# Seven products instead of eight in a feed-forward, inside a pipelined two-layer graph kernel

## The chip, the cores and the metric

The kernel runs on one core of one Trainium2 chip. Its engines each work through a queue of their own: TensorE (PE; its weight loads are shown apart as PEld), VectorE (DVE), ScalarE (ACT), GpSimd (POOL) and SyncE (SP), which here only issues transfers. They wait for each other by semaphores. TensorE writes its results into PSUM, eight banks of 128 partitions x 512 float32; the other engines read them from there. The metric is the device time of one execution in microseconds (us), as the median of several runs.

## The reference: two layers over 64 small graphs

The input is `x` of 64 x 256 x 256 (batch, node, feature) and an integer adjacency `adj` of 64 x 256 x 256. The first layer is two graph attentions, a norm, a feed-forward with Relu, and a norm. The second is attention with eight heads weighted by relation, a norm, a feed-forward with Gelu, and a norm. Cut to what the change touches:

```python
# first layer (weights of layer 0)
h = gat(gat(x, adj, W1, a1), adj, W2, a2)      # softmax over masked scores, then a product
h = layernorm(x + h)
ff = relu(h @ w_ff1 + b_ff1) @ w_ff2 + b_ff2    # 256 -> 1024 -> 256
x = layernorm(h + ff)
# second layer (weights of layer 1)
# ... queries, keys, scores, relation-weighted values ...
x = _ln(src + attn_out, g1, beta1)
ff = jax.nn.gelu(x @ W1 + b1, approximate=False) @ W2 + b2   # x @ W1 is what changes
return _ln(x + ff, g2, beta2)
```

All of it is in float32. The product `x @ W1` is 16384 x 256 by 256 x 1024.

## The kernel before

The batches are taken two at a time: 32 groups of 512 tokens. A turn of the loop works on three groups at once, each at another stage: `y_` is in the second layer, `x_` in the first layer's feed-forward, `z` in the graph attention. The order of TensorE's and SyncE's instructions is the order of the program text; for the other engines a scheduler picks it when the kernel is built. Blocks of 128 tokens are numbered t = 0 to 3, P = 128, F = N = 256, FF = 1024, KB = NB = G = 2, T = 4, FB = 8, TN = 512. `bank()` gives one of six PSUM banks.

The pieces concerned (cuts are marked):

```python
def normed_features(u, l, xn, natural=False, queues=(nc.sync,)):
    # features onto partitions: transposes in 32x32 squares, then 16 placing transfers
    yt = work.tile([P, Q, KB, T, 32], F32, tag="yt", name=f"yt{u}_{l}", bufs=1)
    for t in range(T):
        nc.vector.transpose(yt[:, :, :, t].rearrange("p q k r -> p k q r"),
                            xn[:, t].rearrange("p (k q c) -> p k q c", k=KB, c=32))
    # ... natural: another layout of the same, 16 transfers on SyncE's queue ...
    hT = work.tile([P, Q, KB, T, 32], F32, tag="hT", name=f"hT{u}_{l}")
    for q in range(Q):
        for a in range(Q):
            queues[a % len(queues)].dma_start(hT[q * 32:(q + 1) * 32, a], yt[a * 32:(a + 1) * 32, q])
    return [hT[:, :, k].rearrange("p a t r -> p t a r") for k in range(KB)]

def gat_softmax(u, l, wh, c, w, aT):
    rows = bank(f"rows{name}")
    for t in range(T):
        nc.tensor.transpose(rows[:, t * P:(t + 1) * P], wh[:, t, c:c + 1].to_broadcast([P, P]), ident)
    # ...
    for b in range(G):
        for t in range(b * NB, (b + 1) * NB):
            nc.scalar.activation(s[:, t, :], rows[:, b * N:(b + 1) * N], AF.Identity, bias=wh[:, t, c + 1:c + 2])
        sb = s[:, b * NB:(b + 1) * NB, :].rearrange("p t n -> p (t n)")
        nc.vector.scalar_tensor_tensor(sb, sb, ALPHA, sb, op0=ALU.mult, op1=ALU.max)
        nc.scalar.activation(sb, sb, AF.Exp)
        for t in range(b * NB, (b + 1) * NB):
            nc.vector.scalar_tensor_tensor(s[:, t, :], s[:, t, :], 1.0, aT[:, t, :], op0=ALU.mult, op1=ALU.mult,
                                           accum_out=z[:, t:t + 1])
    nc.vector.reciprocal(z, z)
    # ...
    for t in range(T):
        nc.scalar.activation(wh[:, t, :w], wh[:, t, :w], AF.Copy, scale=z[:, t:t + 1])
    return s

def gat_first(u, s, xp):                        # products hpp
    for t in range(T):
        # ... two matmuls of 258 columns into a bank ...
        nc.scalar.copy(hp[:, t, :WH], ps[:, :WH])

def normed(u, l, y, blocks=range(T)):
    # ...
    for t in blocks:
        nc.vector.bn_stats(st[:, t, :], y[:, t, :])
        nc.vector.bn_aggr(mv[:, t, :], st[:, t, :])
    nc.gpsimd.tensor_scalar(rs[:, bt], mv[:, bt, 1], EPS, 0.0, op0=ALU.add, op1=ALU.add)
    nc.gpsimd.tensor_tensor(rs[:, bt], rs[:, bt], mhalf[:, bt], ALU.pow)
    nc.vector.scalar_tensor_tensor(nm[:, bt], mv[:, bt, 0], -1.0, rs[:, bt], op0=ALU.mult, op1=ALU.mult)
    for t in blocks:
        nc.scalar.activation(y[:, t, :], y[:, t, :], AF.Identity, bias=nm[:, t:t + 1], scale=rs[:, t:t + 1])
    # ...

def affine(y, g_, b_):
    nc.vector.tensor_mul(y, y, g_[:, None, :].to_broadcast(list(y.shape)))
    nc.vector.tensor_add(y, y, b_[:, None, :].to_broadcast(list(y.shape)))

def hidden(u, l, hT, wi, bi, func, blocks, h1=None):   # h1p: 8 banks a group, 2 matmuls of 512 columns each
    # ...
    for f in blocks:
        ps = bank(f"h1p{u}_{l}_{f}")
        for k in range(KB):
            nc.tensor.matmul(ps, wi[:, k, f * P:(f + 1) * P], hT[k], start=(k == 0), stop=(k == KB - 1))
        nc.scalar.activation(h1[:, f, :], ps, func, bias=bi[:, f:f + 1])
    return h1
```

`hidden_out` and `hidden_out_block` are the second product of a feed-forward (`yfp`): per block of tokens 8 matmuls of 256 columns, and after two blocks VectorE adds the bank to `y`. The second half of a turn:

```python
    # ... attention of y_, first_hidden of x_ in between; load_x(z + 1) ...
    out_(0)
    piece()
    if Z:
        project(z)
    out_(1)
    if Z:
        first_scores(z)                      # rows and the first softmax
    normed(y_, 2, y)
    if X:
        hT = normed_features(y_, 2, y, queues=(nc.sync, nc.scalar))
        affine(X["y"], rg1, rb1)
    else:
        piece()
        hT = to_features(y, f"h3T{y_}")
    affine(y, rg3, rb3)
    if X:
        hidden_out(x_, 0, X["y"], X["h1"], wf2)
        normed(x_, 1, X["y"])
    if waiting:
        finish(*waiting.pop(), 0, G)         # the output norm of the group before, and its transfer
    if Z:
        checked(z, Z["aq"])
    if z + 1 < NG:
        load_adjacency(z + 1)
    if Z:
        Z["hp"] = gat_first(z, Z["s"], Z["xp"])
    h1 = hidden(y_, 1, hT, w1, b1, AF.Gelu, range(FB))
    if X:
        X["hT"] = (normed_features(x_, 1, X["y"], natural=True) if Z else to_features(X["y"], f"h2T{x_}"))
        affine(X["y"], rg2, rb2)
    if Z:
        second_scores(z)                     # rows and the second softmax
    # ... the last two turns put off the rest ...
    for t in range(T):
        if t == T - 1:
            second_sums(z)
        hidden_out_block(y_, 1, y, h1, w2, t)
    waiting.append((y_, y))
```

Of the kernel before, what the change touches and what calls it, by code (L numbers as in the profile page):

```python
# [16 lines left out]
P = 128  # L17
# [368 lines left out]
def narrow_path(  # L386
# [171 lines left out]


# [9 lines left out]
    def scaled(w, scale):  # L569
        for k in range(KB):  # L570
            nc.gpsimd.tensor_scalar(w[:, k], w[:, k], scale[:, k:k + 1], 1.0, op0=ALU.mult, op1=ALU.mult)

    def folding():

        shifted(wf1, range(FB // 2), lb1, bf1, "bf1")
        yield
        shifted(wf1, range(FB // 2, FB), lb1, bf1, "bf1")
        scaled(wf1, lg1)
        yield
        for w, bias, name in ((wq, bq, "bq"), (wk, bk, "bk")):  # L580
            shifted(w, range(KB), lb2, bias, name)
            scaled(w, lg2)
        yield
        ps = bank("rbvp")
        for k in range(KB):
            nc.tensor.matmul(ps, lb2[:, k:k + 1].to_broadcast([P, P]), wv[:, k].rearrange("p r f -> p (r f)"),
                             start=(k == 0), stop=(k == KB - 1))
        nc.vector.tensor_tensor(rbv, rbv, ps, ALU.add)
        scaled(wv.rearrange("p c r f -> p c (r f)"), lg2)
        shifted(w1, range(FB // 2), lb3, b1, "b1")  # L590
        yield
        shifted(w1, range(FB // 2, FB), lb3, b1, "b1")
        scaled(w1, lg3)
        yield
# [6 lines left out]


# [16 lines left out]
    def normed_features(u, l, xn, natural=False, queues=(nc.sync,)):  # L619


        yt = work.tile([P, Q, KB, T, 32], F32, tag="yt", name=f"yt{u}_{l}", bufs=1)
        for t in range(T):
            nc.vector.transpose(yt[:, :, :, t].rearrange("p q k r -> p k q r"),  # L624
                                xn[:, t].rearrange("p (k q c) -> p k q c", k=KB, c=32))
        if natural:
            hT = work.tile([P, KB, TN], F32, tag="hT", name=f"hT{u}_{l}")
            to = hT.rearrange("c k (t a r) -> c (k t) a r", a=Q, r=32)
            for q in range(Q):
                for a in range(Q):  # L630
                    nc.sync.dma_start(to[q * 32:(q + 1) * 32, :, a],
                                      yt[a * 32:(a + 1) * 32, q].rearrange("c k t r -> c (k t) r"))
            return [hT[:, k] for k in range(KB)]
        hT = work.tile([P, Q, KB, T, 32], F32, tag="hT", name=f"hT{u}_{l}")
        for q in range(Q):
            for a in range(Q):
                queues[a % len(queues)].dma_start(hT[q * 32:(q + 1) * 32, a], yt[a * 32:(a + 1) * 32, q])
        return [hT[:, :, k].rearrange("p a t r -> p t a r") for k in range(KB)]
# [29 lines left out]
    def gat_softmax(u, l, wh, c, w, aT):  # L668

        name = f"{u}_{l}"  # L670
        rows = bank(f"rows{name}")
        for t in range(T):
            nc.tensor.transpose(rows[:, t * P:(t + 1) * P],  # L673
                                wh[:, t, c:c + 1].to_broadcast([P, P]), ident)
        s = work.tile([P, T, N], F32, tag="s", name=f"s{name}")
        z = work.tile([P, T], F32, tag="z", name=f"z{name}")
        for b in range(G):
            for t in range(b * NB, (b + 1) * NB):
                nc.scalar.activation(s[:, t, :], rows[:, b * N:(b + 1) * N], AF.Identity,  # L679
                                     bias=wh[:, t, c + 1:c + 2])  # L680
# [9 lines left out]
        for t in range(T):  # L690
            nc.scalar.activation(wh[:, t, :w], wh[:, t, :w], AF.Copy, scale=z[:, t:t + 1])
        return s

    def gat_first(u, s, xp):
        hp = work.tile([P, T, WX], F32, tag="wh", name=f"hp{u}")
        for t in range(T):
# [19 lines left out]
    def normed(u, l, y, blocks=range(T)):  # L716
# [14 lines left out]
        for t in blocks:  # L731
            nc.scalar.activation(y[:, t, :], y[:, t, :], AF.Identity, bias=nm[:, t:t + 1],  # L732
                                 scale=rs[:, t:t + 1])
# [8 lines left out]
    def hidden(u, l, hT, wi, bi, func, blocks, h1=None):  # L742
# [9 lines left out]
        return h1  # L752

# [103 lines left out]

    def first_scores(z):
        d = g[z]
        d["s"] = gat_softmax(z, 0, d["xp"], F + 2, WH, d["aT"])  # L860

    def second_scores(z):
        d = g[z]
        d["s"] = gat_softmax(z, 1, d["hp"], F, F, d["aT"])
# [24 lines left out]
    def finish(u, y, b, n):  # L889
# [3 lines left out]
        affine(y[:, bt, :], rg4, rb4)  # L893
# [6 lines left out]
    def turn(y_, x_, z):  # L900
# [52 lines left out]
        if Z:  # L953
            first_scores(z)
        normed(y_, 2, y)
        if X:
            hT = normed_features(y_, 2, y, queues=(nc.sync, nc.scalar))
            affine(X["y"], rg1, rb1)
        else:
            piece()  # L960
            hT = to_features(y, f"h3T{y_}")
        affine(y, rg3, rb3)
        if X:
            hidden_out(x_, 0, X["y"], X["h1"], wf2)
            normed(x_, 1, X["y"])
        if waiting:
            finish(*waiting.pop(), 0, G)
# [4 lines left out]
        if Z:  # L972
            Z["hp"] = gat_first(z, Z["s"], Z["xp"])
        h1 = hidden(y_, 1, hT, w1, b1, AF.Gelu, range(FB))
        if X:
            X["hT"] = (normed_features(x_, 1, X["y"], natural=True) if Z
                       else to_features(X["y"], f"h2T{x_}"))
            affine(X["y"], rg2, rb2)
        if Z:
            second_scores(z)  # L980
        if y_ >= NG - 2:
# [100 lines left out]
```

## Time and profile before

| | before |
|---|---|
| median of three runs | 3218.24 us (3218.14 to 3224.62) |
| profiled execution, span | 3218.0 us |
| mean granted TensorE clock | 0.994 |
| instructions | 44167 |

In the profile, a group of instructions is named by line, engine, operation and the tiles it writes and reads, as `h1p<-hT,w`: the product `h1p` from features `hT` and weights `w`. `128x512` is partitions by elements. "[1.62 <-POOL rs L728]" means that the engine sat idle for 1.62 us before, and that GpSimd's write of `rs` at line 728 ended the wait. Times in a timeline are from the start of the span, and several instructions in a row are merged, with their count as `x8`. An instruction that only issues a transfer stands under SPq or ACTq. Matmuls overlap, so a row's duration reaches past the start of the next row; from start to start is what a row costs.

Two groups of the page, which are the two feed-forward products of the second layer:

```profile
L760 PE MATMUL yfp<-w,h 128*128 128x256 f32 x2048 | 452.9, 379 | 0.0
...
L749 PE MATMUL h1p<-hT,w 128*128 128x512 f32 x992 | 430.8, 592 | 0.0
```

After the names come the count, the busy time in us and the mean of one in ns, and the engine's idle time before them.

### The profile page before, as it was taken

How to read it: one execution, taken by the hardware profiler on the slowest of the kernel's cores; microseconds unless marked ns; L12 is line 12 of the kernel's file. 1: busy time of each engine (PE TensorE's matmuls, PEld its weight loads, DVE VectorE, ACT ScalarE, POOL GpSimd, SP SyncE). 2: the span in 40 equal slices, each digit the busy share in tenths (PEclk: the TensorE clock that was granted, in tenths of full speed). 3: DMA queues.
4: the chain of work that ended last, by engine and by line, in shares of the span. 5: the costliest groups of instructions: out<-in, count | busy, mean ns of one | idle time of the engine just before them, and what ended most of it. 6: DMA issues, size and time to landing. Idle time of an engine off the chain costs nothing.

```text
span 3218.0 us, 44167 instructions
## 1 busy us (share of the span) xinstructions
PE 3175.9 (99%) x16816; PEld 2040.2 (63%) x16816; DVE 1958.3 (61%) x3550; ACT 1432.6 (45%) x2756; POOL 193.6 (6%) x381
## 2 busy tenths in 40 slices
PE   8999999999999999999999999999999999999998
PEld 5566656566666666665666665666666665656655
DVE  3556666555675666665656665566665666655555
ACT  4344444444444444434444444444344444444432
POOL 1000000000000000000000000000000000000000
PEclk9999999999999999999999999999999999999999
DMA  5011111121111221111211112211112111111100
GB/s 143 20 40 40 34 38 33 42 46 31 41 28 40 46 45 29 41 32 40 47 33 40 34 33 46 46 29 42 30 40 46 40 33 38 34 42 34 25 16 15
DMA packets 473050, 125.08 MB, mean 39 GB/s; under 512 B 401368, under 2 KB 472192, under 8 KB 472832
## 3 DMA queue, kind: packets, MB, share of 16 engines
q1 hardware_dynamic: 459520, 112.71, 16.0%
q10 hardware_dynamic: 12256, 8.43, 0.9%
q8 instruction: 136, 2.23, 0.3%
q0 software_dynamic: 1056, 1.05, 0.1%
q14 instruction: 82, 0.67, 0.1%
HBM read 57.04 MB, written 16.78 MB: 23 GB/s over the span
## 4 chain that ended last, share of the span: by engine, by line
PE 97%; DVE 1%; DMA 1%; ACT 0%; POOL 0%; issue 0%; SPq 0%; ACTq 0%; POOLq 0%; DVEq 0%
PE h1p L749 28%; PE yfp L760 27%; PE po L829 7%; PE vp L792 7%; PE sp L808 4%; PE yop L711 4%; PE qp L779 3%; PE xpp L663 3%; PE kp L779 3%; PE hpp L700 3%; PE ygp L711 3%; PE zo L832 2%; PE rows L673 1%; DVE rz L837 0%; ACT y L732 0%; DMA rg<-in_L_gnn_g_ln_dram 0%
## 5 line engine op out<-in xcount | busy, mean ns | idle before, releaser
L816 DVE TENSOR_TENSOR ea<-e,aT 128x1024 f32<-128x1024 f32 x256 | 302.2, 1222 | 333.7 <-ACT e L814 333.7
L751 ACT ACTIVATE h<-h1p,cols 128x512 f32<-128x512 f32 x512 | 338.9, 691 | 348.6 <-PE h1p L749 348.2
L732 ACT ACTIVATE y<-y,nm,rs 128x256 f32<-128x256 f32 x512 | 265.3, 588 | 442.3 <-DVE nm L729 436.4
L760 PE MATMUL yfp<-w,h 128*128 128x256 f32 x2048 | 452.9, 379 | 0.0
L749 PE MATMUL h1p<-hT,wf 128*128 128x512 f32 x992 | 450.6, 602 | 0.0
L760 PE MATMUL yfp<-wf,h 128*128 128x256 f32 x2048 | 447.4, 379 | 0.0
L749 PE MATMUL h1p<-hT,w 128*128 128x512 f32 x992 | 430.8, 592 | 0.0
L760 PEld LDWEIGHTS yfp<-wf,h 128*128 128x128 f32 x2048 | 387.0, 190 | 51.9 <-issue 0.5
L760 PEld LDWEIGHTS yfp<-w,h 128*128 128x128 f32 x2048 | 386.6, 190 | 52.3 <-issue 0.8
L814 ACT ACTIVATE e<-sp 128x512 f32<-128x512 f32 x512 | 263.8, 602 | 224.4 <-PE sp L808 218.0
L749 PEld LDWEIGHTS h1p<-hT,w 128*128 128x128 f32 x992 | 188.4, 190 | 224.2 <-issue 200.7
L749 PEld LDWEIGHTS h1p<-hT,wf 128*128 128x128 f32 x992 | 180.6, 189 | 228.8 <-issue 193.1
L837 DVE RECIPROCAL rz<-zo 128x512 f32<-128x512 f32 x64 | 214.7, 3354 | 53.5 <-PE zo L832 53.5
L682 DVE SCALAR_TENSOR_TENSOR s<-s 128x512 f32<-128x512 f32 x128 | 87.1, 680 | 242.6 <-ACT s L679 241.3
L792 PE MATMUL vp<-wv,hT 128*128 128x512 f32 x480 | 214.0, 599 | 0.0
L624 DVE STREAM_TRANSPOSE yt<-y 128x256 f32<-128x256 f32 x368 | 152.4, 433 | 83.5 <-ACT y L732 77.8
L725 DVE BATCH_NORM_STATS2 st<-y 128x6 f32<-128x256 f32 x512 | 193.2, 409 | 4.4
L739 DVE TENSOR_TENSOR y<-y,rg 128x1024 f32<-128x1024 f32 (+1 forms) x130 | 156.3, 1202 | 9.3 <-ACT y L732 6.0
L792 PEld LDWEIGHTS vp<-wv,hT 128*128 128x128 f32 x480 | 88.7, 190 | 110.4 <-issue 103.2
L740 DVE TENSOR_TENSOR y<-y,rb 128x1024 f32<-128x1024 f32 (+1 forms) x130 | 156.5, 1204 | 3.3
L727 POOL TENSOR_SCALAR rs<-mv 128x4 f32<-128x4 f32 (+1 forms) x130 | 31.1, 248 | 2084.0 <-DVE mv L726 2076.7
L819 DVE TENSOR_TENSOR es<-e 128x1024 f32<-128x1024 f32 x128 | 156.0, 1219 | 0.0
(155 smaller groups left out, 3561.8 us busy)
## 6 DMA issues: line engine op xcount, KB each, us to landing
hT<-yt SPq DMA_DIRECT2D x1224, 32.0 KB, 1.9
y<-in_x_dram SPq DMA_DIRECT2D x32, 512.0 KB, 4.0
xq<-in_x_dram SPq DMA_DIRECT2D x240, 64.0 KB, 2.4
aq<-in_adj_dram SPq DMA_DIRECT2D x240, 64.0 KB, 2.5
out_dram<-y SPq DMA_DIRECT2D x30, 512.0 KB
hT<-yt ACTq DMA_DIRECT2D x248, 32.0 KB, 1.9
wf<-in_L_gnn_w_ff_dram SPq DMA_DIRECT2D x2, 1024.0 KB, 7.1
w<-in_L_gnn_W_dram SPq DMA_DIRECT2D x2, 1024.0 KB
```

The lines of the kernel that those rows point to most:

```text
L711: nc.tensor.matmul(ps[:, i * F:(i + 1) * F], lhs(t, k), rhs(b, k), start=(k == 0), stop=(k == n - 1))
L725: nc.vector.bn_stats(st[:, t, :], y[:, t, :])
L732: nc.scalar.activation(y[:, t, :], y[:, t, :], AF.Identity, bias=nm[:, t:t + 1], scale=rs[:, t:t + 1])
L749: nc.tensor.matmul(ps, wi[:, k, f * P:(f + 1) * P], hT[k], start=(k == 0), stop=(k == KB - 1))
L751: nc.scalar.activation(h1[:, f, :], ps, func, bias=bi[:, f:f + 1])
L760: nc.tensor.matmul(ps[:, i * F:(i + 1) * F], h1[:, k, t * P:(t + 1) * P], wo_[:, k, :], start=(k == 0), stop=(k == FB - 1))
L779: nc.tensor.matmul(ps, w[:, k, m * P:(m + 1) * P], hT[k], start=(k == 0), stop=(k == KB - 1))
L792: nc.tensor.matmul(ps, hT[k][:, t * P:(t + 1) * P], wvf[:, k, :], start=(k == 0), stop=(k == KB - 1))
L814: nc.scalar.activation(e[:, a, :], ps[a], AF.Exp, scale=isd)
L816: nc.vector.tensor_tensor(ea[:, a:a + 2, :], e[:, a:a + 2, :], ab[:, None, :].to_broadcast([P, 2, NB * N]), ALU.mult)
L829: nc.tensor.matmul(po[hp, m * N:(m + 1) * N], vs[:, hp], w[:, a, j * N:(j + 1) * N], start=(n == 0), stop=(n == len(terms) - 1))
L837: nc.vector.reciprocal(rz, zo)
```

## The change

The first product of the second feed-forward is done by Strassen's scheme, in the form with four sums on each side and running totals. The weights (256 x 1024) are cut into quarters by input half and output half, the features (256 x 512) into quarters by input half and batch. Seven products of such quarters and some additions give the four quarters of the result, instead of eight products. The weight sums are made once, by GpSimd, at the start. In each turn VectorE makes four differences of feature quarters; the products go into four PSUM banks (two for each half `h` of an output quarter); ScalarE copies some of the intermediate sums out, VectorE adds them to others on the way to `h1`, and later products are added in the same banks (`start` false). Gelu then works on `h1` in place for three of the quarters. The two matmul groups of `gat_first`, which stood ahead of the product, are put between its last parts.

The rest is order. Instructions inside `behind(name)` are to be issued after the last instruction marked with that name: the first softmax behind the transposes and transfers of the features, the norm of the first feed-forward behind the copies out of the banks, the output norm behind the second softmax. Lastly, GpSimd places the four diagonal blocks of the transposed features, so that 12 transfers are left of 16.

```diff
+    def seven(w, name):
+        h = FF // 2
+        a11, a12, a21, a22 = (w[:, k, o * h:(o + 1) * h] for o in range(2) for k in range(2))
+        s1, s2, s4 = (const.tile([P, h], F32, name=f"{name}s{n}") for n in (1, 2, 4))
+        nc.gpsimd.tensor_tensor(s1, a21, a22, ALU.add)
+        nc.gpsimd.tensor_tensor(s2, s1, a11, ALU.subtract)
+        nc.gpsimd.tensor_tensor(s4, a12, s2, ALU.subtract)
+        nc.gpsimd.tensor_tensor(a21, a11, a21, ALU.subtract)
+        return a11, a12, a22, s1, s2, a21, s4
 ...
         scaled(w1, lg3)
+        w1s.extend(seven(w1, "w1"))
 ... normed_features:
+        n = 0
         for q in range(Q):
             for a in range(Q):
-                queues[a % len(queues)].dma_start(hT[q * 32:(q + 1) * 32, a], yt[a * 32:(a + 1) * 32, q])
+                to, at = hT[q * 32:(q + 1) * 32, a], yt[a * 32:(a + 1) * 32, q]
+                if q == a:
+                    nc.gpsimd.tensor_copy(to, at)
+                else:
+                    mark["placed"] = queues[n % len(queues)].dma_start(to, at)
+                    n += 1
 ... gat_softmax is cut in two (score_rows, and the rest); gat_first takes a range of blocks
+    def hidden_seven(u, l, hT, w, bi, func, h1):
+        a11, a12, a22, s1, s2, s3, s4 = w
+        # tt: the differences; cp: the copies; quarter[k][b]; moving(n): difference n; sub, out, product
+        sub(0, quarter[0][1], quarter[0][0])
+        sub(1, quarter[1][1], moving(0))
+        sub(2, quarter[1][1], quarter[0][1])
+        sub(3, quarter[1][0], moving(1))
+        # copied: ScalarE, bank to cp; added: VectorE, h1 quarter = bank one[h] + copy; done: func on 256 columns
+        for h in halves:
+            two[h] = bank(f"h1b{u}_{l}_{h}")
+            product(two[h], h, a12, quarter[1][0], True)
+            c = copied(h, 0, two[h])
+            one[h] = bank(f"h1a{u}_{l}_{h}")
+            product(one[h], h, a11, quarter[0][0], True)
+            added(h, 0, 0, c)
+        yield
+        for h in halves:
+            product(two[h], h, s1, moving(0), True)
+            p5[h] = copied(h, 1, two[h])
+        for h in halves:
+            product(two[h], h, s4, quarter[1][1], False)
+            copied(h, 0, two[h])
+        yield
+        for h in halves:
+            product(one[h], h, s2, moving(1), False)
+            added(h, 0, 1, cp[:, 2 * h, :])
+            # func on both of the half's rows of h1, 512 columns each
+        yield
+        for h in halves:
+            product(one[h], h, s3, moving(2), False)
+            added(h, 1, 1, p5[h])
+        yield
+        for h in halves:
+            product(one[h], h, a22, moving(3), False)
+            done(h, 1, 0, one[h])
+            done(h, 1, 1)
 ... turn:
         if Z:
-            first_scores(z)
+            first_rows(z)
         normed(y_, 2, y)
         if X:
             hT = normed_features(y_, 2, y, queues=(nc.sync, nc.scalar))
+        if Z:
+            with behind("transposed", "placed"):
+                first_softmax(z)
 ...
             hidden_out(x_, 0, X["y"], X["h1"], wf2)
-            normed(x_, 1, X["y"])
-        if waiting:
-            finish(*waiting.pop(), 0, G)
+        h1 = work.tile([P, FB, TN], F32, tag="h1", name=f"h1{y_}_1", bufs=1)
+        for n, _ in enumerate(hidden_seven(y_, 1, hT, w1s, b1, AF.Gelu, h1)):
+            if Z and n > 1:
+                Z["hp"] = gat_first(z, Z["s"], Z["xp"], Z.get("hp"), range(2 * n - 4, 2 * n - 2))
+        if X:
+            with behind("copied"):
+                normed(x_, 1, X["y"])
+            X["hT"] = (normed_features(x_, 1, X["y"], natural=True) if Z
+                       else to_features(X["y"], f"h2T{x_}"))
+            with behind("added"):
+                affine(X["y"], rg2, rb2)
 ... checked, load_adjacency
-            Z["hp"] = gat_first(z, Z["s"], Z["xp"])
-        h1 = hidden(y_, 1, hT, w1, b1, AF.Gelu, range(FB))
-        if X:
-            X["hT"] = (normed_features(x_, 1, X["y"], natural=True) if Z
-                       else to_features(X["y"], f"h2T{x_}"))
-            affine(X["y"], rg2, rb2)
         if Z:
             second_scores(z)
+        if waiting:
+            with behind("scaled" if Z else "copied"):
+                finish(*waiting.pop(), 0, G)
```

## The prediction, made before the result was known

> **What bounds the kernel now.** I read the page's busy times first, then the chain that ended last:
>
> ```profile
> PE 3175.9 (99%) x16816; PEld 2040.2 (63%) x16816; DVE 1958.3 (61%) x3550; ACT 1432.6 (45%) x2756; POOL 193.6 (6%) x381
> ...
> PE 97%; DVE 1%; DMA 1%; ACT 0%; POOL 0%; issue 0%; SPq 0%; ACTq 0%; POOLq 0%; DVEq 0%
> ```
>
> TensorE is the end of nearly every wait. A busy TensorE need not be a full one, so I next looked at one whole turn of the loop (32 turns, each working on three groups of two batches at once), by windows:
>
> ```profile
> 1528.18:1626.12 97.94, 97.94 (x522) 62.86 (x520) 61.07 (x110) 44.65 (x86) 5.63 (x11) 1.00 0.18 38
> ```
>
> The columns are the stretch, its length, then busy time of PE, PEld, DVE, ACT and POOL, the granted clock, the DMA share and GB/s. TensorE has work for all 97.94 us at clock 1.00. The turns repeat to 0.01 us in the list of the chain in order of time. So a turn costs exactly what its matmuls cost, and the other engines have room on average (DVE 61 of 98 us). The TensorE timeline gives the price of each matmul form:
>
> ```profile
> 1526.46 1.89 PE L711 MATMUL yop<-wo,q 128*128 128x256 f32 x8
> 1528.18 0.60 PE L673 MATMUL rows<-ident,xp 128*128 128x128 f32 x4
> 1528.62 13.98 PE L760 MATMUL yfp<-wf,h 128*128 128x256 f32 x64
> 1542.44 3.64 PE L700 MATMUL hpp<-xp,s 128*128 128x258 f32 x16
> 1545.92 13.90 PE L749 MATMUL h1p<-hT,w 128*128 128x512 f32 x32
> 1559.65 0.60 PE L673 MATMUL rows<-ident,hp 128*128 128x128 f32 x4
> 1560.09 10.53 PE L760 MATMUL yfp<-w,h 128*128 128x256 f32 x48
> ```
>
> Columns: start, duration, engine, line, operation, count. From start to start: 64 records of 256 columns take 1542.44 - 1528.62 = 13.82 us, 215.9 ns each; 32 records of 512 columns take 1559.65 - 1545.92 = 13.73 us, 429.1 ns each. Each float32 matmul of the program is two records. The second feed-forward's first product is the row at 1545.92: 16 matmuls, 13.73 us of every turn.
>
> **What the Trainium skill says.**
> - "FP8 and Floating Point Precision", TensorE Precision Notes: true FP32 is four passes through the array. "TensorE: Matmul & The Clock Gate", "Wait — 56ns, not 53.3ns?": a warm pass takes N / 2.4 GHz + about 2.5 ns. The trace agrees: a record is two passes, 2 x 256 / 2.4 = 213.3 ns against 215.9, and 2 x 512 / 2.4 = 426.7 against 429.1. So the extra is per record, and halving the columns costs almost nothing.
> - "ScalarE: Activation LUTs", "What ACT_TABLE_LOAD costs": about 1283 ns a load. The trace has 1283 ns, some 62 times: Gelu once and Exp once a turn. The new order of ScalarE still has two a turn.
> - "SBUF — State Buffer", "SBUF: two separate sides": a VectorE instruction with two SBUF inputs and a GpSimd instruction lock each other out of a shared port pair. No row of this trace shows it; the new GpSimd copies stand beside such VectorE work.
>
> **The change part by part.**
> (1) Seven products instead of eight. Each quarter product is 512 outputs by 128 inputs by 256 tokens: 4 matmuls of 256 columns. 7 x 4 = 28 matmuls, 56 records x 215.9 ns = 12.09 us. Against 13.73 us that is 1.64 us a turn; times 32 turns 52.5 us, 1.6% of 3218. This is the ceiling: no other TensorE work leaves. Getting below 3154 us (2%) would take 64 us.
>
> (2) Additions. VectorE gets per turn 4 differences of 128x256 (424 ns in the like row of the softmax) and 6 additions of 128x512 from PSUM (about 685 ns): 1.7 + 4.1 = 5.8 us. ScalarE gets 6 copies of 128x512 (about 0.60 us) and its 8 Gelus of 512 become 4 of 512 and 8 of 256: some 4 to 5 us more. GpSimd gets four small copies at each of the two feature transposes. In sum all fits (DVE 67, ACT 49 of 96 us). What counts is whether it fits within the 12 us of the products, because the running sums live in four banks that TensorE may only write again once they are read.
>
> (3) The start. The products now come right after hidden_out, where before gat_first (1542.44 to 1545.92) stood between. So the normed features must be in place 3.5 us sooner. Before:
>
> ```profile
> 1537.20 0.42 DVE L624 STREAM_TRANSPOSE yt<-y 128x256 f32<-128x256 f32 x1
> ...
> 1537.65 5.01 ACTq L637 DMA_DIRECT2D hT<-yt  x8
> ...
> 1537.68 5.29 SPq L637 DMA_DIRECT2D hT<-yt  x8
> ```
>
> The last block is issued at about 1542.4 and lands 1.9 us later, 1544.3: too late for the new order. This is what the queueing is for. Without the softmax in between, VectorE's statistics of the last block end at about 1530.1, GpSimd's power and the scale take 1.8 us (as before: 1531.2 to 1533.04), ScalarE's four rows to 1534.0, the last transpose to 1534.5. 12 transfers over two queues are 6 x 0.62 = 3.7 us of issue, and with 1.9 us landed by about 1540.2. That is 2 us ahead of 1542.44. The four GpSimd copies (a 128x256 tensor_scalar takes about 0.48 us there) end earlier. So the start is hidden.
>
> (4) The softmax behind it. ScalarE is held by its own six transfer issues until 1538.3, then rows, VectorE, Exp, VectorE, ScalarE's scaling until about 1544.6. First copy out of a bank until 1545.2; TensorE wants that bank again at 1542.44 + 16 x 0.2159 = 1545.89. Enough, with 0.6 us to spare.
>
> (5) The middle, where I expect the loss. The second products (s1) are copied by ScalarE while TensorE does the other half, 4 x 0.2159 = 0.86 us. The copy needs 0.2 us from the end of the matmul (as in h1p to Gelu before) plus 0.60 plus some 0.06 back: 0.86. No slack, and a late weight load cannot be prefetched: I allow 0.1 to 0.2 us a turn.
> Then VectorE. After the softmax its queue holds, in the order of the built program: the differences, five statistics, the addition of hidden_out's second half, two statistics, the first addition of the new product, then two small scale rows (nm) for the norm of the first feed-forward and for the output norm, and only then the other half's addition. Worked along with the durations of before: the softmax and differences end at 1543.7, the statistics at 1545.7, addition and statistics at 1547.4 (1.69 us, as from 1542.64). The nm rows wait for GpSimd's two powers:
>
> ```profile
> 1544.03 0.30 DVE L726 BATCH_NORM_AGGREGATE mv<-st 128x2 f32<-128x6 f32 x2
> 1545.95 0.16 DVE L729 SCALAR_TENSOR_TENSOR nm<-mv,rs 128x4 f32<-128x4 f32 x1 [1.62 <-POOL rs L728]
> 1546.93 0.16 DVE L729 SCALAR_TENSOR_TENSOR nm<-mv,rs 128x4 f32<-128x4 f32 x1 [0.82 <-POOL rs L728]
> ...
> 1544.89 2.01 POOL L728 TENSOR_TENSOR rs<-rs,mhalf 128x4 f32<-128x4 f32 x2
> ```
>
> The reader is to see that the second nm starts 2.6 us after the statistics end (1544.33), because one power of 128x4 takes 1.0 us. So the other half's addition starts at 1547.4 + 2.6 = 1550.0 and ends at 1550.7. TensorE wants to write that bank at 1542.44 + 36 x 0.2159 = 1550.2: 0.5 us of waiting, with 0.1 for the restart 0.6 us a turn.
>
> (6) After it gat_first's blocks (1.74 us each pair) stand between the last products and cover the remaining additions; rows, second softmax (scaled by about 1568 against a need at 1569.4) and the transposed features (landed about 1574 against 1576) keep 1 to 2 us each. No loss.
>
> (7) Ends. At the start GpSimd puts the first of four weight sums (128x512, about 1.3 us by its 128x256 additions of 0.72) ahead of a power that the first turn waits for, and the other three before the next: about 1.5 us lost once. The last two turns have no gat_first to fill, and the last also waits for the Gelus: they gain about 1 and 0.5 us instead of 1.64.
>
> Sum: 30 turns x (1.64 - 0.15 - 0.6) = 26.7; last two 1.5; start -1.5. 3218.2 - 26.7 = 3191.5, taken as 3190 us.
>
> **The rivals.**
> (a) All hidden: VectorE is at the addition 0.6 us sooner than I put it. Then 3218 - 52 + 2 = 3168 us. For it: the author queued things just for this, and every step of mine is an estimate to some tenths. Against: two nm rows in front of an addition that TensorE waits for.
> (b) VectorE or ScalarE late everywhere: if the port lock of GpSimd's copies, or the softmax behind six transfers, pushes VectorE back by 1 us more, the wait grows to 1.6 us a turn and the gain is gone: 3215 to 3222 us.
> (c) The features land after 1542.44. Each us late costs 32 us. Against: 2 us to spare.
> (d) Rounding of many small waits (some 15 new ones a turn, each 0.05 us when just met): another 10 us, inside the range.
>
> **Range and chances.** 3190 us, 3170 to 3209 in 8 of 10: the low end is nearly all hidden, the high end a wait of 1.2 us a turn. Faster by over 2% is beyond the ceiling of 52.5 us: 0.02. Slower by over 2% needs 3.7 us of new waiting a turn: 0.03. Within 2%: 0.95.
>
> **What would show it.** In the timeline of a turn: the products' records add up to 12.1 us, a turn lasts about 97.0 us instead of 97.94, and the one gap of half a us or more is before the s2 product's second half, released by VectorE's addition, with nm rows waiting for GpSimd right before it. The first product starts with no gap and no wait for a transfer. If the turn lasts 96.3 us, rival (a) holds; if it starts with a gap on hT, (c). The prediction is wrong if records of 256 columns take other than 216 ns here, or if a second place loses more than 0.3 us a turn.

## The result and the profile after

The changed kernel takes 3190.94 us (median of 4 runs, 3190.37 to 3193.16); the kernel before, on the same chip, 3218.97. The ratio is 0.9911, 95% interval 0.9893 to 0.9928: 0.9% faster. The profiled execution spans 3188.7 us, against 3218.0 before.

The chain that ended last:

```profile
PE 91%; DVE 4%; ACT 1%; POOL 1%; DMA 1%; ACTq 1%; issue 1%; SPq 0%; DVEq 0%; POOLq 0%
```

PE's share of the chain fell from 97% to 91%. Where TensorE alone used to set the end, it now waits in places for VectorE, ScalarE and GpSimd. Two turns by windows (columns as before: stretch, length, busy PE, PEld, DVE, ACT, POOL, clock, DMA share, GB/s):

```profile
1802.67:1899.25 96.58, 96.58 (x546) 67.17 (x544) 65.98 (x120) 48.25 (x96) 12.49 (x19) 1.00 0.17 36
1899.25:1997.13 97.88, 96.90 (x545) 67.09 (x544) 65.88 (x120) 48.15 (x96) 12.48 (x19) 1.00 0.17 36
```

Before, every turn took 97.94 us. Now most take 96.58, but eight take 96.8 to 97.9. The first of these two, in the timeline of TensorE:

```profile
1803.11 13.98 PE L878 MATMUL yfp<-wf,h 128*128 128x256 f32 x64
1816.92 1.03 PE L820 MATMUL h1b<-hT,w 128*128 128x256 f32 x4
...
1820.38 1.89 PE L820 MATMUL h1b<-tt,w1s 128*128 128x256 f32 x8
1822.10 1.97 PE L820 MATMUL h1b<-hT,w1s 128*128 128x256 f32 x8
1823.91 2.10 PE L820 MATMUL h1a<-tt,w1s 128*128 128x256 f32 x8
1825.85 1.90 PE L736 MATMUL hpp<-xp,s 128*128 128x258 f32 x8
```

Read the distances from start to start. A product of eight records (four matmuls) should take 8 x 0.2159 = 1.73 us. The products on sums are named after their weights: s1 (1820.38) takes 1.72, s4 (1822.10) 1.81, s2 (1823.91) 1.94. So s4 loses 0.08 us and s2 0.22. TensorE has no idle time before s4: its first weight load had to wait for ScalarE's copy and began at 1822.08, 0.03 us ahead of its matmul, and the first record then took 0.30 us from start to start instead of 0.22. The first product follows the feed-forward at 1816.92 without a gap, and everything after s2 is on time. What VectorE and GpSimd do just then:

```profile
1821.16 0.30 DVE L762 BATCH_NORM_AGGREGATE mv<-st 128x2 f32<-128x6 f32 x2
1821.37 0.67 DVE L830 TENSOR_TENSOR h<-h1a,cp 128x512 f32<-128x512 f32 x1
...
1822.01 2.01 POOL L764 TENSOR_TENSOR rs<-rs,mhalf 128x4 f32<-128x4 f32 x2
...
1823.07 0.16 DVE L765 SCALAR_TENSOR_TENSOR nm<-mv,rs 128x4 f32<-128x4 f32 x1 [1.03 <-POOL rs L764]
...
1824.05 0.16 DVE L765 SCALAR_TENSOR_TENSOR nm<-mv,rs 128x4 f32<-128x4 f32 x1 [0.82 <-POOL rs L764]
1824.13 0.69 DVE L830 TENSOR_TENSOR h<-h1a,cp 128x512 f32<-128x512 f32 x1
```

VectorE adds the first half at 1821.37, idles 1.03 and 0.82 us for GpSimd's two powers, and only then adds the other half, until 1824.82. TensorE wants to write that bank at 1816.92 + 36 x 0.2159 = 1824.69; the rest of the 0.22 us is again a late weight load (1824.88), after which the first record took 0.32 us.

The second of the two turns is slower for another reason. ScalarE's own transfers, in the slow turn and in the ordinary one:

```profile
1808.91 3.73 ACTq L667 DMA_DIRECT2D hT<-yt  x6
...
1812.68 1.57 ACT L714 ACTIVATE s<-rows,xp 128x256 f32<-128x256 f32 x4 [4.28 <-DMA hT<-yt]
...
1905.48 5.03 ACTq L667 DMA_DIRECT2D hT<-yt  x6
...
1910.56 1.57 ACT L714 ACTIVATE s<-rows,xp 128x256 f32<-128x256 f32 x4 [5.59 <-DMA hT<-yt]
```

The six issues take 5.03 us instead of 3.73, the softmax starts 1.3 us late, and VectorE's whole queue with it. What moved in the stretch 1906.7 to 1908 of the slow turn beside the transfers that place the features (packets, MB, share of 16 engines):

```profile
q8 instruction: 1, 0.02, 5.8%
```

One packet of instructions, 16 KB (the page counts 141 of them with 2.31 MB), holds one of the 16 DMA engines for 0.058 x 16 x 1.3 = 1.2 us, amid those transfers. By the packets' start times an instruction packet falls 6.3 to 10.1 us after the turn's rows in six of the eight turns that exceed 96.7 us (in one of them, of 96.79 us, a packet of 8 KB of another queue), and in none of the turns of 96.58. That is agreement in time; no run takes the packets away. In five of the six ScalarE is held longer and starts the softmax 0.2 to 1.3 us late. In the sixth (97.69 us, packet at 10.1) it starts on time, but a transfer that SyncE issued at 9.0 lands after 3.59 us instead of 1.9, and VectorE's first difference waits for the transfers:

```profile
2494.64 0.43 DVE L803 TENSOR_TENSOR tt<-hT 128x256 f32<-128x256 f32 x1 [0.95 <-DMA hT<-yt]
```

The other two turns (96.80 and 96.88 us) stay open: their softmax is 0.2 and 0.3 us late too, with no packet among the transfers before it. The eight lose 6.1 us together.

Where the 29.3 us between the two profiles come from:

| stretch | before, us | after, us | difference |
|---|---|---|---|
| up to the rows of the first full turn | 157.10 | 158.57 | +1.5 |
| 29 turns | 2840.11 | 2806.88 | -33.2 |
| from the rows of turn 29 to the end | 220.8 | 223.3 | +2.5 |

Within the first row chance plays a part: the first feed-forward's second product happens to start 1.4 us sooner (76.49 against 77.89). From there to the first full turn the change loses 82.08 - 79.21 = 2.9 us. Of these, 2.15 us lie before TensorE's transposes of the first group, which start 8.48 us after the b1 shift (TensorE's `b1sp`) instead of 6.33: GpSimd's first weight sum (1.26 us) stands ahead of its power, which starts 1.1 us later, and VectorE's nm then takes 1.22 us beside the second sum, where it takes 0.16 alone:

```profile
96.76 1.26 POOL L566 TENSOR_TENSOR w1s<-w1s,w 128x512 f32<-128x512 f32 x1
96.81 1.22 DVE L765 SCALAR_TENSOR_TENSOR nm<-mv,rs 128x4 f32<-128x4 f32 x1 [2.10 <-POOL rs L764]
```

The other 0.7 us are qp's, which works at half clock for longer there (5.66 us from start to start, 4.95 before). At the end of the changed kernel the largest wait that is new is in turn 30 (TensorE and ScalarE):

```profile
3084.72 1.58 ACT L768 ACTIVATE y<-y,nm,rs 128x256 f32<-128x256 f32 x3
...
3086.32 1.28 ACT L861 ACT_TABLE_LOAD   x1
...
3093.10 2.57 ACT L768 ACTIVATE y<-y,nm,rs 128x256 f32<-128x256 f32 x5
3093.76 0.77 PE L633 MATMUL h2T31p<-ident,y 128*128 128x128 f32 x5 [3.59 <-ACT y L768]
3094.87 5.40 PE L897 MATMUL qp<-h2T,wq 128*128 128x512 f32 x8 [0.35 <-DVE h2T L634]
```

Three of the norm's rows run right behind the copies. The fourth stands behind a table load and all twelve Gelu instructions; TensorE idles 3.59 us for it, and then works on qp at half clock, 5.40 us instead of 3.67 before.

### The profile page after: what moved, and what is told of

It is laid out like the page before. It is cut to its first block, busy times and chain, and to the rows that moved or that the text cites. A ratio compares the mean times of both kernels' runs of the same rounds, so it can differ in the third digit from the quotient of the medians.

```text
span 3188.7 us, 46935 instructions
## 1 busy us (share of the span) xinstructions
PE 3137.3 (98%) x17584; PEld 2178.4 (68%) x17584; DVE 2117.7 (66%) x3870; ACT 1547.8 (49%) x3076; POOL 412.1 (13%) x633
## 3 DMA queue, kind: packets, MB, share of 16 engines
q8 instruction: 141, 2.31, 0.3%
## 4 chain that ended last, share of the span: by engine, by line
PE 91%; DVE 4%; ACT 1%; POOL 1%; DMA 1%; ACTq 1%; issue 1%; SPq 0%; DVEq 0%; POOLq 0%
PE yfp L878 24%; PE h1p L785 14%; PE po L947 7%; PE vp L910 7%; PE h1a L820 6%; PE sp L926 4%; PE h1b L820 4%; PE qp L897 4%; PE yop L747 4%; PE kp L897 3%; PE hpp L736 3%; PE xpp L694 3%; PE ygp L747 3%; PE zo L950 2%; POOL rs L764 1%; DVE st L761 1%
## 5 line engine op out<-in xcount | busy, mean ns | idle before, releaser
L932 ACT ACTIVATE e<-sp 128x512 f32<-128x512 f32 x512 | 263.7, 603 | 224.4 <-PE sp L926 218.1
L787 ACT ACTIVATE h<-h1p,cols 128x512 f32<-128x512 f32 x256 | 172.8, 692 | 239.0 <-PE h1p L785 239.0
L665 POOL COPY hT<-yt 32x256 f32<-32x256 f32 x248 | 215.8, 870 | 191.9 <-DVE yt L648 166.1
L826 ACT COPY cp<-h1b 128x512 f32<-128x512 f32 x192 | 111.1, 581 | 113.4 <-PE h1b L820 70.1
L830 DVE TENSOR_TENSOR h<-h1a,cp 128x512 f32<-128x512 f32 x192 | 130.3, 682 | 45.7 <-PE h1a L820 45.6
L696 ACT COPY xp<-xpp 128x260 f32<-128x260 f32 x128 | 47.6, 373 | 232.6 <-PE xpp L694 232.5
```

Of the source, the lines that this page charges most:

```text
L665: nc.gpsimd.tensor_copy(to, at)
L932: nc.scalar.activation(e[:, a, :], ps[a], AF.Exp, scale=isd)
```

## The experiments

The theory: the saving is the seven products alone (1.64 us a turn, ideal turn 96.30); the rest is waits of in-order queues, each with its own cause: VectorE's nm rows before s2, ScalarE held by its transfers, the norm at the end, the weight sums at the start. The rivals stand with each run. Times of turns and stretches are those of the profiled execution. All ratios are against the kernel before on the same chip. "Start" is the time from the first feed-forward's second product to the rows of the first full turn, "end" from the rows of turn 29 to the last instruction. One of e9's four executions was slow (4092.74 us) and is left out of its ratio.

| run | median, us | ratio, 95% interval | ordinary turn | start | end |
|---|---|---|---|---|---|
| before | 3218.97 | 1 | 97.94 | 79.2 | 220.8 |
| changed | 3190.94 | 0.9911 [0.9893, 0.9928] | 96.58 | 82.1 | 223.3 |
| e1_scales_last | 3183.11 | 0.9885 [0.9868, 0.9901] | 96.37 | 81.9 | 224.4 |
| e2_split_8_4 | 3183.83 | 0.9886 [0.9869, 0.9902] | 96.37 | 82.4 | 224.2 |
| e3_tail_norm | 3188.43 | 0.9901 [0.9885, 0.9918] | 96.58 | 82.0 | 219.1 |
| e4_eight | 3234.84 | 1.0047 [1.003, 1.0064] | 98.28 | 79.4 | 225.2 |
| e5_sums_later | 3193.41 | 0.992 [0.9903, 0.9936] | 96.58 | 81.9 | 225.9 |
| e6_unqueued | 3217.51 | 0.9994 [0.9985, 1.0003] | 97.6 to 97.9 | 82.4 | 225.3 |
| e7_sixteen | 3204.18 | 0.9951 [0.9935, 0.9968] | 97.00 | 82.5 | 224.6 |
| e8_all | 3179.15 | 0.9878 [0.9862, 0.9895] | 96.37 | 81.9 | 223.9 |
| e9_sums_queued | 3194.55 | 0.9915 [0.9895, 0.9935] | 96.60 | 82.0 | 224.4 |
| e10_best | 3174.25 | 0.9858 [0.9841, 0.9874] | 96.37 | 81.8 | 219.1 |
| e11_eight_interleaved | 3223.46 | 1.001 [1.0003, 1.0017] | 97.94 | 78.9 | 224.7 |
| e12_norm_unqueued | 3332.35 | 1.0347 [1.033, 1.0364] | 100 to 103 | 82.0 | 222.5 |

**The wait before s2: e1_scales_last.**

```diff
-            with behind("scaled" if Z else "copied"):
+            with behind("scaled" if Z else "copied", "added"):
                 finish(*waiting.pop(), 0, G)
```

> The changed kernel with one thing moved: the output norm of the group before (its statistics and its nm row on VectorE) may only be issued after the last addition of the products. Theory (the s2 wait is VectorE's queue: five statistics and a second nm row that waits for GpSimd's second power stand ahead of the other half's addition): the wait of 0.22 to 0.24 us before s2's second half goes in every ordinary turn, 96.58 becomes about 96.34 us, and most of the 0.9 us that the turns of 97.7 lose there; the whole about 3180 us (3177 to 3184). Rival (the addition is late because of the products or of ScalarE's copies, not of these rows): the wait stays, 96.6 us a turn and 3190 us. Second rival (the output norm, moved behind, delays the features of the next turn): a new gap at qp, over 3190 us.

Measured: 96.37 us in every ordinary turn, and 96.54 to 96.76 in four with an instruction packet. TensorE around s2:

```profile
1819.33 1.89 PE L820 MATMUL h1a<-tt,w1s 128*128 128x256 f32 x8
1821.05 1.90 PE L736 MATMUL hpp<-xp,s 128*128 128x258 f32 x8
```

s2 now takes 1821.05 - 1819.33 = 1.72 us: the wait is gone, as the theory said, and no new one came at qp. The changed kernel shows the same by itself: its first full turn, which has no output norm yet and so one nm row less there, takes 96.37 us. The total missed the range's middle by 3 us because the end was 1.1 us and the start's chance part 1.2 us worse. What is left of the turn is s4's 0.08 us: 96.37 = 96.30 + 0.07.

**ScalarE held by its transfers: e2_split_8_4 and e7_sixteen.** e2 gives SyncE eight transfers and ScalarE four:

```diff
-            hT = normed_features(y_, 2, y, queues=(nc.sync, nc.scalar))
+            hT = normed_features(y_, 2, y, queues=(nc.sync, nc.sync, nc.scalar))
```

> The changed kernel with the 12 placing transfers split 8 to SyncE and 4 to ScalarE instead of 6 and 6. Theory (ScalarE is held by its own issues, and the softmax and all of VectorE's queue start when they end; in the turns of 97.7 us an instruction fetch holds a DMA engine for 1.2 us amid these transfers and ScalarE waits that long): the softmax starts 1.2 us sooner, the s2 wait is gone in ordinary turns (96.34 us) and the turns with a fetch fall to about 96.6; the whole 3178 to 3183 us. Rival (the eight transfers of SyncE land too late for the first product at 14.3 us after the turn's rows): a gap at the first product, up to 1 us in turns with a fetch; 3185 to 3200 us.

Measured: 96.37 us too, by the other way: ScalarE's issues end after 2.44 us, all of VectorE's queue comes sooner, and the s2 wait is gone with the nm rows still in place. Only four turns of 29 exceed 96.40 us (96.43 to 96.95) and the first product shows no gap: the rival fell.

e7 takes GpSimd's placing away; all 16 blocks go by transfer, eight on each queue:

```diff
-                if q == a:
-                    nc.gpsimd.tensor_copy(to, at)
-                else:
-                    mark["placed"] = queues[n % len(queues)].dma_start(to, at)
-                    n += 1
+                mark["placed"] = queues[n % len(queues)].dma_start(to, at)
+                n += 1
```

> The changed kernel with all 16 blocks placed by transfers, 8 and 8, none by GpSimd. Theory (what counts is when ScalarE comes free): its two more issues of 0.6 us make the softmax 1.2 us late in every turn, as a fetch does in the turns of 97.7 us: 97.6 to 97.9 us a turn, the whole 3218 to 3228. Rival (a slack of a microsecond is there, or GpSimd's copies cost as much as they save): 96.6 us a turn, 3190. Second rival (more transfers on the same lanes wait longer for each other): over 98.3 us.

Measured: 97.00 us a turn. The direction is the theory's, the size is not: ScalarE's issues do take 5.01 us and the softmax does start 1.3 us late, but only about 0.5 us of it reaches s1 (whose bank is copied late), and since TensorE itself then comes later to s2, the wait there is gone. A delay early in a chain of waits is partly paid with the later ones; I had added it to them. Without the placing a turn is 0.42 us longer.

**The queueing: e6_unqueued and e12_norm_unqueued.** e6 makes every `behind(...)` of the change empty; e12 takes off one only:

```diff
 # e6, in behind()
-            stack.enter_context(tc.issue_after(mark[n].ins))
+            pass
 # e12, in turn()
-            with behind("copied"):
-                normed(x_, 1, X["y"])
+            normed(x_, 1, X["y"])
```

> The changed kernel without any queueing: seven products, GpSimd's placing and TensorE's order as they are, but softmax and norms issued in the order that the build gives them by itself. Theory (the queueing is what makes the seven products pay): the softmax goes first, the features land 14.6 to 15 us after the turn's rows against a need at 14.3, so a gap of 0.4 to 1 us at the first product; the norm's rows between the copies cost 0.7 as in turn 30 of the run with the norm set free there; a transposition ahead of an addition some more; a turn of 97.7 to 98.8 us, the whole 3220 to 3250. Rival (the queueing hardly matters): under 96.9 us a turn, under 3198.

> The changed kernel with one of its queueings taken off: the norm of the first feed-forward is not held behind the products' copies; softmax and output norm stay queued. Theory (of the queueing it is this one that pays: a row of the norm that waits for GpSimd's power stands on ScalarE ahead of a copy out of the bank that TensorE waits for): 97.5 to 98.0 us a turn, nearly all of what the run without any queueing lost, 3212 to 3222. Rival (the softmax's queueing is the one that pays, by the features' landing): 96.6 to 96.9 us a turn, 3189 to 3197.

Measured: without queueing the seven products bring nothing (0.9994, the interval holds 1), and with the softmax queued but the norm not, the kernel is 3.5% slower than before, more than either of my theories had. In e6 the first product starts on time (14.25 us after the rows); the gap that I expected there does not exist. Both runs lose their time at s1. In e12:

```profile
1907.40 2.01 POOL L764 TENSOR_TENSOR rs<-rs,mhalf 128x4 f32<-128x4 f32 x2
...
1908.66 0.60 ACT L768 ACTIVATE y<-y,nm,rs 128x256 f32<-128x256 f32 x1 [3.95 <-DVE nm L765]
1909.16 0.56 ACT L826 COPY cp<-h1b 128x512 f32<-128x512 f32 x1
...
1909.78 1.13 PE L820 MATMUL h1b<-tt,w1s 128*128 128x256 f32 x4 [2.99 <-ACT cp L826]
```

ScalarE idles 3.95 us in front of a row of the norm that waits for nm, which waits for GpSimd's power. Behind that row in its queue stands the copy that frees TensorE's bank, ready all along. In e6 the same row waits 2.1 to 2.3 us, because there the softmax comes first and the statistics, and with them nm, come sooner: the last ones before nm end 2.0 us after the first product's start, in e12 4.5. So queueing the softmax back makes the norm later, and then the norm has to be queued too. Whether the norm's queueing would be enough without the softmax's was not run; since e6's features are in time, it may be. With the idling half clock comes in e12: spells of it in 24 of the 29 turns, a mean clock of 0.978 against 0.993. Four of the five turns without a spell last 100.3 to 100.5 us (the first, without an output norm, 98.8), those with one 101.2 to 102.9, so the wait by itself costs some 3.7 us a turn.

**What the order is worth alone: e4_eight and e11_eight_interleaved.** Both keep order, queueing and GpSimd's placing and put the old eight products back (the weight sums, which nothing needs then, are left out). e4 runs gat_first after the products, e11 between the last of them as the change does:

```diff
-        for n, _ in enumerate(hidden_seven(y_, 1, hT, w1s, b1, AF.Gelu, h1)):
-            if Z and n > 1:
-                Z["hp"] = gat_first(z, Z["s"], Z["xp"], Z.get("hp"), range(2 * n - 4, 2 * n - 2))
+        # e4:  hidden(y_, 1, hT, w1, b1, AF.Gelu, range(FB), h1); Z["hp"] = gat_first(z, Z["s"], Z["xp"])
+        # e11:
+        for n, f in enumerate((range(6), range(6, 7), range(7, 8))):
+            hidden(y_, 1, hT, w1, b1, AF.Gelu, f, h1)
+            if Z and n < 2:
+                Z["hp"] = gat_first(z, Z["s"], Z["xp"], Z.get("hp"), range(2 * n, 2 * n + 2))
```

> The new order, the queueing and GpSimd's placing with the old eight products (hidden in place of hidden_seven, weight sums left out, norm and affine queued behind the fourth Gelu). Theory (the saving is the seven products alone, the order only makes room for them): a turn of 97.94 us as before, 3215 to 3220 us. Rival (the order itself saves something, for instance at the ends): under 3212 us. Rival (the order costs something that Strassen's products pay back): over 3223 us.

> The new order with the old eight products once more, but gat_first's blocks between the last products as in the changed kernel, instead of right ahead of the rows that need their copies. Theory (the 0.35 us a turn that the first such run lost is that copy alone, and the saving of the change is the products alone): 97.94 us a turn, 10 us less than that run, 3222 to 3227 (the end still has the norm behind the Gelus). Rival (the order costs the 0.35 us elsewhere): 98.28 us a turn, 3233 to 3236.

Measured: e4's turn is 98.28 us, because gat_first now stands right before the rows that need its last copy (rows takes 0.79 us from start to start instead of 0.43). e11's turn is 97.94, the turn of before to the hundredth:

```profile
1820.34:1918.28 97.94, 97.94 (x522) 62.86 (x521) 61.88 (x110) 44.93 (x86) 12.46 (x19) 1.00 0.17 36
```

The order by itself brings nothing and costs nothing in the turns. All that a turn gains, 97.94 - 96.58, is the products'. And both runs, which have no weight sums, have the start of before (79.4 and 78.9), but a long end (225.2 and 224.7): the end's loss belongs to the order and not to the products.

**The start: e5_sums_later and e9_sums_queued.** e5 calls the weight sums in the first turn instead of before it; e9 also forbids them to pass the powers:

```diff
-        w1s.extend(seven(w1, "w1"))            # in folding(), before the first turn
+        if not w1s:                            # in turn(), after scores(0)
+            with behind("powered"):            # e9 only: mark of GpSimd's last power
+                w1s.extend(seven(w1, "w1"))
```

> The changed kernel with GpSimd's four weight sums issued in the first turn, whose products need them some 80 us later, instead of before it. From the start of the first feed-forward's second product to the rows of the first full turn the changed kernel takes 82.1 us and the kernel before 79.2. Theory (GpSimd's first sum of 1.26 us stands ahead of one power, the others ahead of the next, and TensorE idles for it and then runs longer at half clock): 79.2 to 79.6 us, the whole some 2.7 us less than the changed kernel, about 3188. Rival (the loss comes from something else in the new start, or the clock alone): 81 us or more, 3190 to 3192.

> As the run before with the sums later, where the build hoisted them back to the old place; here they may only be issued behind the second of the two powers of the start. From the start of the first feed-forward's second product to the rows of the first full turn the changed kernel takes 82.1 us, the kernel before 79.2. Theory (a sum of 1.26 us stands ahead of each power): 79.2 to 79.8 us, the whole 2.5 us less than the changed kernel, 3187 to 3189. Rival (something else in the start, or the half clock, which lasts 13.7 us there instead of 10.2): 81 us or more, 3190 to 3193.

Measured: neither gains. In e5 the sums run where they ran in the changed kernel (the first at 94.50 us, there at 94.54): the scheduler put them forward, although the text has them later. In e9 they do come behind the powers, and TensorE's transposes of the first group start 6.33 us after the b1 shift as in the kernel before, not 8.48. But the sums then lie beside VectorE's norm rows (e9, VectorE and GpSimd):

```profile
102.70 1.48 POOL L565 TENSOR_TENSOR w1s<-w 128x512 f32<-128x512 f32 x1
102.98 1.22 DVE L764 SCALAR_TENSOR_TENSOR nm<-mv,rs 128x4 f32<-128x4 f32 x1
```

The first norm's nm, ahead of the sums, takes 0.16 us, this one 1.22 us beside a sum: the loss has only moved on to the second norm. One of two scalings by rg takes 1.95 instead of 1.22 us, and the sums themselves up to 2.25 instead of 1.26. VectorE's copies of the transposes come 1.2 us later than before, and qp then runs at half clock for longer (6.5 us from start to start, 4.95 before). e4 and e11 show that the sums are what the start loses to; where they would cost nothing, these two runs did not find.

**The end: e3_tail_norm.**

```diff
-            with behind("copied"):
+            with behind(*(["copied"] if Z else [])):
                 normed(x_, 1, X["y"])
```

> The changed kernel with the norm of the last group's first feed-forward, in turn 30 alone, not queued behind the products' copies. Theory (5.4 us of the end are lost because its rows stand on ScalarE behind the table load and the eight Gelus, 3.7 us at the transposes h2T31 and 1.7 us in qp at half clock after that idling): 3185 to 3187 us, the wait of 3.6 us before h2T31p gone. Rival (the rows now delay the copies of the products in that turn and the loss only moves into the products; or the half clock comes anyway): 3189 to 3192 us.

Measured: the wait at h2T31 is gone, qp takes 3.5 us from start to start, and the end is 219.1 us, 4.2 less. The rival is partly right: the rows now stand between the copies, and TensorE waits 0.35 and 0.33 us for them. The profiled span is only 1.3 us shorter than the changed kernel's (3187.4), because the first full turn happens to begin 2.7 us later; the median of 3188.43 lies between the two ranges.

**Together: e8_all and e10_best.** e8 is e1, e2, e3 and e5 at once. e10 is e1, e2 and e9, and instead of e3 it writes the norm of turn 30 between the copies and the Gelus:

```diff
+            if X and not Z and n == 1:       # in the loop over hidden_seven
+                with behind("copied"):
+                    normed(x_, 1, X["y"])
```

> The changed kernel with four things at once: the output norm behind the last addition, transfers 8 and 4, the norm free in turn 30, the weight sums in the first turn. Theory (the losses are separate): turns of 96.37 us, also those with a fetch (11.9 us less than the changed kernel), start 2.7 less, end 4.2 less: 18.8 us less, 3170 to 3174. Rival (the ways overlap, one loss only gives place to another): 3176 to 3182.

> All that helped, mended: the output norm behind the last addition, transfers 8 and 4, the sums behind the powers, and in turn 30 the norm's four rows between the copies and the Gelus instead of free among the copies. Theory (the losses are separate): turns of 96.37 us as in the run of all four, start 2.7 us less, no wait of 3.6 us at h2T31 and none at the copies in turn 30: 3169 to 3175. Rival (at the end, time saved before one wait is idled away at the next one and at half clock): 3176 to 3180 as the run of all four.

Measured: both have 96.37 us in all 29 turns, also in those with an instruction packet. e8 missed by 5 us: e5 was no gain, and its end is 223.9, with waits of 0.66 and 0.33 us at the copies and half clock for 13.6 us (e3: 6.8). e10 reaches 3174.25 us, the fastest of all, 1.4% under the kernel before (0.9858) and within its range, though the 2.7 us that its theory had for the start did not come (81.8 against 82.1); its turn by windows:

```profile
1798.37:1894.73 96.36, 96.36 (x545) 67.25 (x544) 65.90 (x120) 48.25 (x96) 12.52 (x19) 1.00 0.17 36
```

## Why the prediction was right, and where it was not

The total fits within 1 us, but partly because two misses cancel: the 29 turns saved 33.2 us where 29 x 0.89 = 25.8 were reckoned, and the start and the end lost 1.4 + 4.9 = 6.3 us more than reckoned.

1. Seven products, 56 records of 215.9 ns: right. Between e11 (97.94) and e1 (96.37) the turn gains 1.57 of 1.64 us.
2. The additions fit: right. VectorE 65.98 and ScalarE 48.25 us of a turn, against the 67 and 49 reckoned.
3. The start of the products is hidden: right, there is no gap. Its reason was half wrong: the queueing is not needed for it. With 12 transfers the features are in time without it (e6), and with 16 they are in time with it (e7); in both the first product starts 14.25 us after the rows. GpSimd's copies take 0.39 us alone, within the 0.48 reckoned, but 1.3 to 1.4 beside VectorE's scalings (see below), and still end in time.
4. The softmax behind the transfers has 0.6 us to spare: right in ordinary turns, where it is even 1.06 us (the first copy ends at 1819.32, its bank is wanted at 1820.38). In the eight others 0.2 to 1.3 us are lost, in the worst 0.4 at h1a and s1 together and 0.9 more than usual at s2. That is rival (b)'s mechanism, in every third turn of the second half, with a cause that I had not thought of. By my own words a second place that loses over 0.3 us a turn would make the prediction wrong; the 0.4 us are over it, but in single turns only.
5. The wait before s2, released by VectorE's addition behind two nm rows: place, cause and neighbours right; e1 and e2 remove it in two ways. The term was mis-sized: 0.22 us instead of 0.6, because the statistics ended 4.5 us after the first product's start (1821.46 - 1816.92) and not 5.0. The 0.1 to 0.2 us allowed for s1's copies came to 0.08, at s4. With the instruction packets the mean turn is 96.79 us, 1.15 saved, against 0.89 predicted.
6. No loss after it: right.
7. The ends: wrong. For the start I had 1.5 us and it is 2.9: the sum ahead of the power is there, but nm beside the next sum (1.1 us more) and the longer half clock (0.7) were not reckoned. For the end I had a gain, 2.4 us from the rows of turn 29 on, and it is a loss of 2.5: I had asked what fills the time without gat_first, but not where the norm queued behind the copies goes when no gat_first covers it. e3 and e10 bring 4.2 us of the 4.9 back.

Rival (a), all hidden in the turns, is what e10 nearly is: 96.37 against 96.30. The port lock that the prediction took from the Trainium skill's "SBUF — State Buffer" ("SBUF: two separate sides") did show, at the placing copies too:

```profile
1808.91 1.23 DVE L775 TENSOR_TENSOR y<-y,rg 128x1024 f32<-128x1024 f32 x1
1809.00 1.39 POOL L665 COPY hT<-yt 32x256 f32<-32x256 f32 x1 [2.91 <-DVE yt L648]
...
1811.77 0.39 POOL L665 COPY hT<-yt 32x256 f32<-32x256 f32 x1
```

The first copy takes 1.39 us beside the scaling by rg, the second 1.30 beside the addition of rb, both instructions with two SBUF inputs; the third takes 0.39 us beside VectorE's addition of `yfp`, which reads one input from PSUM. The page's mean of 0.87 us mixes the two kinds. VectorE loses little by it (the addition of rb takes 1.30 us in 61 of 126 cases, 1.21 to 1.23 before), so rival (b)'s push of 1 us did not come from there. Where it did cost something is nm at the start.

## What to carry to other kernels

When an engine with an in-order queue frees a buffer that another engine waits for, look at what stands ahead of that instruction and at what it waits for itself; one norm's rows let in front of the copies cost 4% here, half clock included (e12 against the changed kernel), and one norm moved behind an addition gained 0.26% (e1). A reordering that pays in the steady loop must be followed into the last turns, where the work that covered it is missing. And before crediting an order, run it with the old work in it: here it was worth nothing by itself (e11), and the new work next to nothing without the queueing (e6).

## What was not expected of the hardware

- Instruction fetches are DMA traffic and seem to reach the critical path. The Trainium skill's "Runtime: NRT & Kernel Launch", section "Instruction fetch mechanics", says that instruction memory is refilled in 16 KiB blocks through a DMA queue of the engine's own. The trace agrees on the block in one instruction queue (2.31 MB in 141 packets); the other moved packets of 8 KB (0.75 MB in 91). What stands beside them in time: a packet of 16 KB holds one DMA engine for 1.2 us, and a transfer issued just before it landed after 3.2 us instead of 1.9. Where the packets fall relative to a turn shifts from turn to turn, so some turns are hit and others not, the longest ones at the same places in the changed kernel, e1 and e3.
- Half clock came in spells of 3.4 us or multiples of it (3.41 to 13.65 us; the last spell of each run is cut off by its end). An idle of 2.4 to 3.6 us at the end of the kernel often brought one, but not always (2.75 us at po brought one in e10 and none in e8): such spells, by estimate 1.7 us lost for each 3.4, make a good part of the difference between the ends in the table. What decides it was not tried.
